# A graph kernel's edge sorter: ranks counted partition by partition, and one index copy for four scatters

## The chip, the cores and the metric

One core of a Trainium2 chip runs the kernel. The metric is the device time of one execution in microseconds (us). The engines named here are PE (matmuls; PEld is its weight loads), DVE (the vector engine), ACT (the scalar engine), POOL (here mostly the issuer of indirect scatters) and SP (the issuer of most transfers). Each engine takes its instructions in program order.

## What is computed

The graph has 12,500 nodes of 64 features and 200,000 edges, which come sorted by destination. Two graph layers follow one another, each with a residual:

```python
edge_index = jnp.stack([src, dst])
h = jnp.maximum(_layernorm(x, axis=-1), 0.0)
x = x + _L0_gnn_ref(h, edge_index, W1l, W1r, b1, W2l, W2r, b2)   # two SAGE convolutions
h = jnp.maximum(_layernorm(x, axis=-1), 0.0)
x = x + _L1_gnn_ref(h, edge_attr_64, src, dst, W1, b1, W2, b2)   # edge messages, mean by sender

def _sage_conv(x, src, dst, Wl, Wr, b):
    agg = jax.ops.segment_sum(x[src], dst, num_segments=N)
    cnt = jax.ops.segment_sum(jnp.ones((src.shape[0],), x.dtype), dst, num_segments=N)
    mean = agg / jnp.maximum(cnt, 1.0)[:, None]
    return mean @ Wl.T + b + x @ Wr.T
# messages: msg = relu([h[src], h[dst], edge] @ W1 + b1) @ W2 + b2, then the mean by src
```

## The kernel before

Nodes are cut into 49 blocks of 256. A *cell* is a pair of a destination block and a source block; there are 49 x 49 = 2401 of them, and each has 128 *slots* for its edges. Gathers and segment sums are matmuls with one-hot matrices, made from a slot's source number and destination number. So every edge first has to be given a slot: its rank among the edges of its cell.

**The stages.** From 0 to 92 us the node features are normalised and the first block is sorted. From 92 to about 1340 us runs the first convolution, with the sorter beside it; up to about 2305 us the second convolution; then two passes over the messages (`last` 0 and 1), with 40 early blocks and 9 late ones. In a convolution the cells go in groups of four (`some_cells`): eight matmuls gather into `got` (L896), ACT copies them to `rows` (L900), DVE makes the one-hot `hot` (L750) from `dcol`, and three groups later eight matmuls add into `acc` (L775). Every sixteen cells DVE makes two `turned` matrices (L741) from `srow`, a row of slot numbers that comes back from memory. When a destination block is complete, `conv` runs its chain over DVE, PE (L834, L839), ACT and DVE (L841).

**The sorter.** `sort(B)` is a generator of 14 steps (`STEPS`), and `sort_to` advances it between groups so that it stays about two blocks ahead; with 49 cells in a block, that is about one step per group. A block's edges lie in a window of 128 partitions x 34 (T = 34, pairs TG = 17). The steps:

- L594 compares the edges' source blocks with the 49 block numbers: a one-hot of 17 x 49 x 2 per partition (1666 elements).
- 17 matmuls (L598) count each column's edges of each cell; a scan and a multiply-add (L602, L603) make running counts, and L606 spreads them over a diagonal (`wide`).
- four pairs of matmuls (L616 with the triangle `lead`, L617 with `wide`) add what lies before an edge in its column and in earlier columns; ACT copies each result to `ranks` (L618), four copies.
- L620, twice, multiplies the one-hot by the source and the destination numbers.
- L625, twice, and L628 take the minimum over the 49 cells: the rank. L630 makes its bf16 copy.
- L635, twice, makes the one-hot of the ranks, `hot_r`. 34 matmuls (L645), with the cells' one-hot as weights (98 columns) and `hot_r` moving (128 columns), put each edge's numbers into its slot; in between L650 and L651 compute `pos`, the row that the edge's term takes in a table in memory.
- ACT copies the result to `rows_o` (L654), three transfers store it, PE transposes it (L663), and ACT writes `scol` and `dcol` (L664, L666).

All PSUM tiles of the sorter have the name `pX`, which has a single bank.

**The scatters.** `edge_terms` transforms edge features and scatters them to tables in memory (`terms`), in units of four tiles of early blocks (U = 4), or three of late ones. It runs as a generator that `Beside` advances at a fixed pace (4.45 per step, later 6.2). Each unit gives eight scatters (or six): for each, DVE copies one column of `pos` to `turn_i` (L381; 16 buffers of one column), and POOL issues an indirect transfer (L382). A unit's scatters go out during the steps of the next unit; those of the last unit of a phase are drained all at once:

```python
for _ in before:
    pass
```

In the message passes POOL also does the subtractions on `hidden` (L1089), which PE's sums (L775) need, and the `terms_in` loads read the tables back.

Of the kernel before, what the change touches and what calls it, by code (L numbers as in the profile page):

```python
# [9 lines left out]
FT = mybir.dt.float32  # L10
BF = mybir.dt.bfloat16
# [103 lines left out]
def fast_path(  # L115
# [239 lines left out]
    def edge_terms(work, psum, groups, ITEMS, U):  # L355
# [17 lines left out]
        def scatter(o, unit):  # L373
            for h in range(2):
                for c, (B, tg, _) in enumerate(unit):
                    assert sorted_blocks() > B
                    t = 2 * tg + h
                    j, n, _ = table_of(B)
                    assert j in cleared
                    at = work.tile([P, 1], I32, name="turn_i", bufs=16)  # L380
                    nc.vector.tensor_copy(at, pos_of(B)[:, t:t + 1])  # L381
                    nc.gpsimd.indirect_dma_start(  # L382
                        out=terms[j][:], out_offset=bass.IndirectOffsetOnAxis(ap=at, axis=0),
                        in_=o[:, c, h], in_offset=None,
                        bounds_check=S * NB * n - 1, oob_is_err=False)
                    yield
# [38 lines left out]
        for _ in before:  # L425
            pass
# [74 lines left out]
    def pos_of(B):  # L501
        return pos[:, B] if B < EARLY else pos_late[:, B - EARLY]
# [3 lines left out]
    def made_cells(work, psum):  # L506
# [8 lines left out]
        with tc.tile_pool(name="made", bufs=1, side="right") as made_in:  # L515
            kexp = made("kexp", [P, NB, 2], BF, [[1, NB], [0, 2]], -NB, 0)
            rexp = made("rexp", [P, S, 2], BF, [[1, S], [0, 2]], 0, 0)
            off = made("off", [P, NB, 1], FT, [[BLK, NB], [0, 1]], -1, 0)

            own = work.tile([P, NB, 2], BF, name="own", bufs=1)  # L520
            even_p = work.tile([P, 1], FT, name="even_p", bufs=1)
            diag_i = made_in.tile([P, NB, 2], I32, name="diag_i")
            nc.gpsimd.iota(diag_i, pattern=[[2, NB], [0, 2]], base=0, channel_multiplier=-1)
            here = made_in.tile([P, NB, 2], FT, name="here")
            nc.vector.tensor_scalar(here, diag_i, 0.0, None, op0=OP.is_equal)
            nc.vector.tensor_reduce(even_p, here.rearrange("p k c -> p (k c)"), AX.X, OP.max)
            nc.vector.tensor_scalar(own, diag_i, -1.0, None, op0=OP.is_equal)
            nc.vector.tensor_add(own, own, here)
            gap_i = made_in.tile([P, P], I32, name="gap_i")
            nc.gpsimd.iota(gap_i, pattern=[[1, P]], base=0, channel_multiplier=-1)  # L530
            lead = work.tile([P, P], BF, name="lead", bufs=1)
            nc.vector.tensor_scalar(lead, gap_i, 0.0, None, op0=OP.is_gt)
            gap = made_in.tile([P, P], BF, name="gap")
            nc.vector.tensor_scalar(gap, ident, -float(S), None, op0=OP.mult)
            nc.vector.tensor_add(lead, lead, gap)
        ones = work.tile([P, P], BF, name="ones", bufs=1)
        nc.vector.memset(ones, 1.0)
        before = [work.tile([2 * NB, TG + 1, 2], BF, name=f"before{n}", bufs=1) for n in range(2)]
        for b in before:
            nc.vector.memset(b, 0.0)  # L540
        flat_ones = work.tile([2 * NB, TG], FT, name="flat_ones", bufs=1)
        nc.vector.memset(flat_ones, 1.0)
        total = work.tile([2 * NB, NB], BF, name="total", bufs=1)
        batch = {}

        def edges_in(B0, B1, queue, i=None):
# [12 lines left out]
            kv, slo, dlo = (work.tile([P, CH, T], BF, name=k)[:, :n] for k in ("kv", "slo", "dlo"))  # L559
# [9 lines left out]
            nc.vector.scalar_tensor_tensor(kv, hi, -float(NB), f[:, 1], op0=OP.add, op1=OP.mult)  # L569
            nc.vector.tensor_scalar(hi, i[:, 0], BLK - 1, None, op0=OP.bitwise_and)  # L570
            nc.vector.tensor_scalar(slo, hi, 1.0, None, op0=OP.add)
            for B in range(B0, B1):
                batch[B] = tuple(t[:, B - B0] for t in (kv, slo, dlo))
# [12 lines left out]
        def flat(a):  # L586
            return a.rearrange("p g k c -> p g (k c)")

        def sort(B):

            kv, slo, dlo = batch[B]
# [4 lines left out]
            many = psum.tile([P, 512], FT, name="pX")  # L596
            for g in range(TG):
                nc.tensor.matmul(many[:2 * NB, g:g + 1], v[:, g, 0].rearrange("p k c -> p (k c)"), ones[:, 0:1],  # L598
                                 start=True, stop=True)
            yield  # L600
            b = before[B % 2]
            nc.vector.tensor_tensor_scan(b[:, 1:, 0], flat_ones, many[:2 * NB, :TG], 0.0, op0=OP.mult, op1=OP.add)  # L602
            nc.vector.scalar_tensor_tensor(b[:, 0:TG, 1], many[:2 * NB, :TG], even_p[:2 * NB], b[:, 0:TG, 0],  # L603
                                           op0=OP.mult, op1=OP.add)
            w = work.tile([2 * NB, TG, NB, 2], BF, name="wide", bufs=1)
            nc.vector.tensor_mul(w, mid(b[:, 0:TG], NB), lead_(own[:2 * NB], TG))  # L606
            nc.vector.tensor_copy(total[:, B:B + 1], b[:, TG, 0:1])


            r = work.tile([P, TG, NB, 2], BF, name="ranks", bufs=1)  # L610
            for n, g0 in enumerate(range(0, TG, 5)):
                yield
                g1 = min(g0 + 5, TG)
                p = psum.tile([P, 512], FT, name="pX")
                q = p[:, :(g1 - g0) * 2 * NB].rearrange("p (g k) -> p g k", k=2 * NB)
                nc.tensor.matmul(q, lead, flat(v[:, g0:g1, 0]), start=True, stop=False)  # L616
                nc.tensor.matmul(q, ones[:2 * NB], flat(w[:, g0:g1]), start=False, stop=True)  # L617
                nc.scalar.copy(flat(r[:, g0:g1]), q)  # L618
                if n % 2:
                    nc.vector.tensor_mul(v[:, :, 1 + n // 2], v[:, :, 0], mid(pairs((slo, dlo)[n // 2]), NB))  # L620
            yield
            k = NB
            for _ in range(2):
                h = k - k // 2
                nc.vector.tensor_tensor(r[:, :, 0:k - h], r[:, :, 0:k - h], r[:, :, h:k], op=OP.min)  # L625
                k = h
            rank = work.tile([P, T], FT, name="rank", bufs=1)
            nc.vector.tensor_reduce(pairs(rank), r[:, :, 0:k].rearrange("p g k c -> p g c k"), AX.X, OP.min)  # L628
            rb = work.tile([P, T], BF, name="rank_b", bufs=1)
            nc.vector.tensor_scalar(rb, rank, float(S), None, op0=OP.add)  # L630
# [9 lines left out]
            for g0, g1, hot in halves:  # L640
                yield

                for g in range(g0, g1):
                    for c in range(2):
                        nc.tensor.matmul(p[:2 * NB, :S], v[:, g, 1:3, :, c].rearrange("p v k -> p (v k)"),  # L645
                                         hot[:, g - g0, :, c], start=g + c == 0, stop=g + c == TG)
                if g0 == 0:
                    j, n, f = table_of(B)
                    q = work.tile([P, T], FT, name="pos_f", bufs=1)
                    nc.vector.scalar_tensor_tensor(q, rank, float(NB), kv, op0=OP.mult, op1=OP.add)  # L650
                    nc.vector.tensor_scalar(pos_of(B), q, float(n), float(n * (S * NB + NB) + f),  # L651
                                            op0=OP.mult, op1=OP.add)
            o = work.tile([2 * NB, S], BF, name="rows_o")
            nc.scalar.copy(o, p[:2 * NB, :S])  # L654
            yield
            n, f = place[B]
            F = len(order[n])
            nc.sync.dma_start(srow_b[B].rearrange("(k s) -> k s", s=S), o[0:NB])
            nc.sync.dma_start(srow_k[n][:, f * S:(f + 1) * S], o[0:NB])
            nc.sync.dma_start(drow_k[n][:, f * S:(f + 1) * S], o[NB:2 * NB])  # L660
            p = psum.tile([P, 512], FT, name="pX")
            pt = p.bitcast(BF)[:, 0:2 * NB]
            nc.tensor.transpose(pt, o, ident_b[:2 * NB, :2 * NB])  # L663
            nc.scalar.copy(scol[:, scol_at[n]:scol_at[n] + NB * F].rearrange("p (k f) -> p k f", f=F)[:, :, f],  # L664
                           pt[:, 0:NB])
            nc.scalar.copy(dcol[:, B * NB:(B + 1) * NB], pt[:, NB:])  # L666
# [17 lines left out]

        p = psum.tile([P, 512], FT, name="pX")
        nc.tensor.matmul(p[:NB, :NB], own[:2 * NB, :, 0], total, start=True, stop=True)
        most = work.tile([NB, 1], FT, name="most", bufs=1)
        nc.vector.tensor_reduce(most, p[:NB, :NB], AX.X, OP.max)
        p = psum.tile([P, 512], FT, name="pX")
        nc.tensor.transpose(p[0:1, :NB], most, ident[:NB, :NB])  # L690
        flag = work.tile([1, 1], FT, name="flag", bufs=1)
        nc.vector.tensor_reduce(flag, p[0:1, :NB], AX.X, OP.max)
        nc.vector.tensor_scalar(flag, flag, S + 0.5, None, op0=OP.is_gt)
        nc.vector.tensor_max(bad, bad, flag)

    STEPS = 14
# [731 lines left out]
```

## Time and profile before

| | |
|---|---|
| median of 3 runs | 3727.71 us (3725.05 to 3731.02) |
| the profiled execution | 3723.96 us, span 3722.1 us, mean granted PE clock 0.991 |
| busy share of the span | PE 94%, PEld 92%, DVE 89%, ACT 69%, POOL 73% |
| L381, index copies | 1360 of early blocks (169.1 us listed), 306 of late ones |
| L382, scatters | 1666, 1937.7 us listed on POOL |
| L618, rank evictions on ACT | 147 of 490 columns (568 ns), 49 of 196 (333 ns) |
| L645, slot matmuls | 1666, 224 ns listed each |

A listed duration of PE or DVE runs from the start of an instruction to its end, and instructions of one engine overlap a little; the distance from one start to the next says how long the engine is held. The profile names, for each wait, the engine and line whose end released it.

### The profile page before, as it was taken

The numbers are of one execution on the slowest core, as the hardware profiler recorded it, in microseconds if no ns is written. First come the engines' busy times: TensorE is split into PE (matmuls) and PEld (weight loads), VectorE is DVE, ScalarE is ACT, GpSimd is POOL, SyncE is SP. The second block draws the span as 40 slices with busy tenths as digits, with TensorE's granted clock in tenths as the row PEclk, the third lists the DMA queues.
The fourth block names the chain that finished last, engine by engine and source line by source line (L and its number), as shares of the span: only waits on it lengthen the run. The fifth ranks groups of instructions, "written<-read, shape, count | busy, mean of one in ns | idle before, by whom it ended". The sixth has DMA issues, their size and how long they took to land.

```text
span 3722.1 us, 130679 instructions
## 1 busy us (share of the span) xinstructions
PE 3505.5 (94%) x51318; PEld 3423.2 (92%) x51318; DVE 3322.8 (89%) x7346; ACT 2568.7 (69%) x5875; POOL 2732.6 (73%) x2306
## 2 busy tenths in 40 slices
PE   1799999999999999999999998999999999998987
PEld 0799999999999999999999998899999999998887
DVE  7899999999999978888888887899999999998998
ACT  3466666666666667777777776688888888876665
POOL 4057787777778777777777774688888888996454
PEclk9999999999999999999999999999999999999999
DMA  6654555555454344444444444666666666666664
GB/s 209 247 169 148 159 153 157 156 157 156 137 166 151 116 129 141 136 136 144 136 131 140 139 132 131 227 215 203 217 214 212 203 216 210 208 196 193 196 213 138
DMA packets 413697, 635.90 MB, mean 171 GB/s; under 512 B 94131, under 2 KB 296247, under 8 KB 413070
## 3 DMA queue, kind: packets, MB, share of 16 engines
q1 hardware_dynamic: 353106, 572.87, 48.7%
q0 software_dynamic: 53312, 51.36, 4.6%
q8 instruction: 402, 6.59, 0.7%
q10 hardware_dynamic: 6652, 3.24, 0.4%
q14 instruction: 225, 1.84, 0.2%
HBM read 474.72 MB, written 155.83 MB: 169 GB/s over the span
## 4 chain that ended last, share of the span: by engine, by line
PE 75%; DVE 15%; DMA 4%; issue 3%; ACT 2%; POOL 1%; SPq 1%; DVEq 0%; POOLq 0%; ACTq 0%
PE acc L775 26%; PE got L896 17%; PE got L1077 11%; PE got L1078 6%; PE pE L414 4%; DVE hot L750 3%; DVE turned L741 2%; PE pE L399 2%; DVE hot_r L635 2%; PE pX L645 2%; DVE turned_d L741 1%; DMA terms_in<-terms 1%; PE acc L839 1%; PE got L1074 1%; PE pX L617 1%
## 5 line engine op out<-in xcount | busy, mean ns | idle before, releaser
L382 POOL DMA_INDIRECT terms<-terms_o,turn_i x1666 | 1937.7, 1163 | 663.3 <-issue 220.5
L900 ACT CAST rows<-got 128x384 bf16<-128x384 f32 x2402 | 1038.5, 487 | 592.3 <-PE got L896 577.7
L775 PEld LDWEIGHTS <-hot 128*128 128x128 bf16 x12006 | 1029.5, 98 | 19.0 <-issue 7.9
L775 PE MATMUL acc<-rows,hot 128*128 128x193 bf16 x9604 | 1006.0, 247 | 0.7 <-DVE hot L750 0.7
L1089 POOL TENSOR_TENSOR hidden<-hidden 128x512 f32<-128x512 f32 (+1 forms) x602 | 756.3, 1257 | 259.6 <-ACT hidden L1086 179.3
L896 PEld LDWEIGHTS <-turned 128*128 128x128 bf16 x9604 | 814.7, 98 | 67.4 <-issue 27.5
L750 DVE TENSOR_TENSOR hot<-dcol,local 128x1024 bf16<-128x1024 bf16 x1202 | 814.3, 682 | 4.1 <-PE acc L775 3.7
L741 DVE TENSOR_SCALAR turned<-srow,nid 128x2048 bf16<-128x2048 bf16 (+1 forms) x906 | 780.4, 875 | 21.1 <-issue 10.7
L1077 PE MATMUL got<-ta,turned 128*128 128x128 bf16 x3920 | 599.8, 220 | 7.3 <-DVE turned L741 7.3
L1077 PE MATMUL got<-tb,turned_d 128*128 128x128 bf16 x3920 | 600.7, 221 | 1.7 <-DVE turned_d L741 1.1
L1078 PE MATMUL got<-tb,turned_d 128*128 128x64 bf16 x3920 | 546.9, 193 | 0.0
L1078 PE MATMUL got<-ta,turned 128*128 128x64 bf16 x3920 | 546.5, 193 | 0.0
L896 PE MATMUL got<-ta,turned 128*128 128x192 bf16 x4802 | 499.7, 247 | 37.4 <-issue 24.8
L1097 ACT ACTIVATE hot_a<-every,scol 128x256 bf16<-128x256 bf16 x1200 | 507.0, 493 | 0.0
L896 PE MATMUL got<-tb,turned 128*128 128x192 bf16 x4802 | 494.1, 246 | 0.8 <-DVE turned L741 0.5
L1086 ACT ACTIVATE hidden<-y 128x512 f32<-128x512 f32 (+1 forms) x301 | 190.4, 632 | 293.5 <-DVE y L1083 169.5
L1077 PEld LDWEIGHTS <-turned 128*128 128x128 bf16 x3920 | 362.8, 98 | 8.2 <-issue 7.8
L1077 PEld LDWEIGHTS <-turned_d 128*128 128x128 bf16 x3920 | 360.2, 98 | 2.9 <-DVE turned_d L741 2.4
L1078 PEld LDWEIGHTS <-turned 128*128 128x128 bf16 x3920 | 359.5, 98 | 1.2
L1078 PEld LDWEIGHTS <-turned_d 128*128 128x128 bf16 x3920 | 359.9, 98 | 0.0
L741 DVE TENSOR_SCALAR turned_d<-drow,nid 128x2048 bf16<-128x2048 bf16 (+2 forms) x302 | 324.9, 1117 | 0.0
L1099 ACT ACTIVATE hot_a<-hot_a 128x1024 bf16<-128x1024 bf16 x300 | 317.2, 1057 | 9.5
(227 smaller groups left out, 5302.4 us busy)
## 6 DMA issues: line engine op xcount, KB each, us to landing
srow<-srow_b SPq DMA_DIRECT2D x300, 512.0 KB
srow<-srow_k SPq DMA_DIRECT2D x149, 512.0 KB
drow<-drow_k SPq DMA_DIRECT2D x149, 512.0 KB
terms_in<-terms SPq DMA_DIRECT2D x294, 160.0 KB
edges<-in_edge_attr_dram SPq DMA_DIRECT2D x200, 192.0 KB
terms<-tb SPq DMA_DIRECT2D x200, 160.0 KB
terms<-tb SPq DMA_DIRECT2D x48, 640.0 KB
terms<-terms_o,turn_i POOLq DMA_INDIRECT x1666
```

What stands on the lines that cost most here:

```text
L382: nc.gpsimd.indirect_dma_start(out=terms[j][:], out_offset=bass.IndirectOffsetOnAxis(ap=at, axis=0), in_=o[:, c, h], in_offset=None, bound ...
L741: nc.vector.tensor_scalar(o[:, h, :n * S], r[:, :n * S], nid[:, h:h + 1], None, op0=OP.is_equal)
L750: nc.vector.tensor_tensor(o[:, :n], cols.rearrange("p (g c) -> p g c", c=2).unsqueeze(2).to_broadcast([P, n, 2 * P, 2]), local.rearrange(" ...
L775: nc.tensor.matmul(self.acc[B][:, h, :W3], lt, r[:, c, 0:W3], start=k + h == 0, stop=k == row - 1 and h == 1, skip_group_check=True)
L896: nc.tensor.matmul(p[:, (i - c) * D3:(i - c + 1) * D3], t[:, h, (a - c0 + i) * S:(a - c0 + i + 1) * S], table[:, (a + i) % NB, h], start=h ...
L900: nc.scalar.copy(g[:, c:c + m, :D3], p[:, :m * D3].rearrange("p (c d) -> p c d", c=m))
L1077: nc.tensor.matmul(p[:, c], lt, rt[:, 0:2 * D], start=i == 0, stop=False, skip_group_check=True)
L1078: nc.tensor.matmul(p[:, c, 0:D], lt, rt[:, 2 * D:], start=False, stop=i == 3, skip_group_check=True)
L1086: nc.scalar.activation(w[:, :n, 0:D], y[:, :n], AF.Relu)
L1089: nc.gpsimd.tensor_sub(w[:, :n, (i + 1) * D:(i + 2) * D], w[:, :n, j], upper(w)[:, :n, j])
L1097: nc.scalar.activation(q[:, c - k], every, AF.Abs, scale=-1.0, bias=scol[:, scol_at[last] + a + c:scol_at[last] + a + c + 1])
L1099: nc.scalar.activation(q[:, :n - k], q[:, :n - k], AF.Relu, bias=1.0, scale=-2.0)
```

## The change

The sorter now ranks an edge in another order: first all edges of its cell in earlier partitions, then those before it in its own partition.

- The 17 counting matmuls and the four pairs become 17 matmuls with the triangle `lead` as weights and the cells' one-hot moving (98 columns), all summed into one PSUM tile: how many edges of each cell lie in earlier partitions. `ahead_p` is that sum over the two columns of a pair, read from PSUM by DVE.
- Within a partition, DVE compares each edge's key with the 33 keys before it. The keys lie in a buffer of 67 columns, 33 of padding and 34 of keys, and `earlier` is an overlapping view of it. Edges outside the block get the key 8192, which takes one more instruction per seven blocks.
- The product of one-hot and `ahead_p` and the comparisons lie side by side in `ranks` (49 + 33 pairs); three halving adds and a reduce sum them. A running maximum (`most`) replaces the counts for the overflow test.
- In the slot matmuls the weights are now `hot_r` (128 columns), and the cells' one-hot moves (98 columns). The result comes out transposed, so `scol` and `dcol` are written at once and the transpose makes `rows_o`. The three transfers are issued in the same step as that transpose.
- A block takes 13 steps instead of 14.
- For early blocks, one DVE copy takes the four columns of a half unit, and four scatters read it; late blocks keep a copy for each scatter. The last unit's scatters are yielded one by one.

```diff
         def scatter(o, unit):
             for h in range(2):
-                for c, (B, tg, _) in enumerate(unit):
+                B0, t = unit[0][0], 2 * unit[0][1] + h
+                if B0 < EARLY:
+                    four = work.tile([P, len(unit)], I32, name="turn_i", bufs=4)
+                    nc.vector.tensor_copy(four, pos[:, B0:B0 + len(unit), t])
+                for c, (B, _, _) in enumerate(unit):
...
-                    at = work.tile([P, 1], I32, name="turn_i", bufs=16)
-                    nc.vector.tensor_copy(at, pos_of(B)[:, t:t + 1])
+                    if B0 < EARLY:
+                        at = four[:, c:c + 1]
+                    else:
+                        at = work.tile([P, 1], I32, name="turn_i", bufs=16)
+                        nc.vector.tensor_copy(at, pos_of(B)[:, t:t + 1])
...
         for _ in before:
-            pass
+            yield
...
+        def earlier(a):
+            (row, _), (step, _) = a.ap
+            return bass.AP(a.tensor, a.offset, [[row, P], [2 * step, TG], [step, T - 1], [step, 2]])
...
-            many = psum.tile([P, 512], FT, name="pX")
+            p = psum.tile([P, 512], FT, name="pX")
+            q = p[:, :2 * NB].rearrange("p (k c) -> p k c", c=2)
             for g in range(TG):
-                nc.tensor.matmul(many[:2 * NB, g:g + 1], v[:, g, 0].rearrange("p k c -> p (k c)"), ones[:, 0:1],
-                                 start=True, stop=True)
+                nc.tensor.matmul(q, lead, v[:, g, 0], start=g == 0, stop=g == TG - 1)
+            r = work.tile([P, TG, KE, 2], BF, name="ranks", bufs=1)
+            nc.vector.tensor_tensor(r[:, :, NB:], mid(pairs(kv), T - 1), earlier(keyed), op=OP.is_equal)
             yield
-            b = before[B % 2]
-            nc.vector.tensor_tensor_scan(b[:, 1:, 0], flat_ones, many[:2 * NB, :TG], 0.0, op0=OP.mult, op1=OP.add)
-            nc.vector.scalar_tensor_tensor(b[:, 0:TG, 1], many[:2 * NB, :TG], even_p[:2 * NB], b[:, 0:TG, 0],
-                                           op0=OP.mult, op1=OP.add)
-            w = work.tile([2 * NB, TG, NB, 2], BF, name="wide", bufs=1)
-            nc.vector.tensor_mul(w, mid(b[:, 0:TG], NB), lead_(own[:2 * NB], TG))
-            nc.vector.tensor_copy(total[:, B:B + 1], b[:, TG, 0:1])
-            r = work.tile([P, TG, NB, 2], BF, name="ranks", bufs=1)
-            for n, g0 in enumerate(range(0, TG, 5)):
-                yield
...
-                nc.tensor.matmul(q, lead, flat(v[:, g0:g1, 0]), start=True, stop=False)
-                nc.tensor.matmul(q, ones[:2 * NB], flat(w[:, g0:g1]), start=False, stop=True)
-                nc.scalar.copy(flat(r[:, g0:g1]), q)
-                if n % 2:
-                    nc.vector.tensor_mul(v[:, :, 1 + n // 2], v[:, :, 0], mid(pairs((slo, dlo)[n // 2]), NB))
+            nc.vector.tensor_mul(v[:, :, 1], v[:, :, 0], mid(pairs(slo), NB))
             yield
-            k = NB
-            for _ in range(2):
+            ahead_p = work.tile([P, NB, 2], BF, name="ahead_p", bufs=1)
+                nc.vector.tensor_reduce(ahead_p, q.unsqueeze(2).to_broadcast([P, NB, 2, 2]), AX.X, OP.add)
+            nc.vector.tensor_mul(r[:, :, 0:NB], v[:, :, 0], lead_(ahead_p, TG))
+            yield
+            nc.vector.tensor_mul(v[:, :, 2], v[:, :, 0], mid(pairs(dlo), NB))
+            yield
+            k = KE
+            for n in range(3):
                 h = k - k // 2
-                nc.vector.tensor_tensor(r[:, :, 0:k - h], r[:, :, 0:k - h], r[:, :, h:k], op=OP.min)
+                nc.vector.tensor_tensor(r[:, :, 0:k - h], r[:, :, 0:k - h], r[:, :, h:k], op=OP.add)
                 k = h
-            rank = work.tile([P, T], FT, name="rank", bufs=1)
-            nc.vector.tensor_reduce(pairs(rank), r[:, :, 0:k].rearrange("p g k c -> p g c k"), AX.X, OP.min)
+                if n == 1:
+                    yield
             rb = work.tile([P, T], BF, name="rank_b", bufs=1)
-            nc.vector.tensor_scalar(rb, rank, float(S), None, op0=OP.add)
+                nc.vector.tensor_reduce(pairs(rb), r[:, :, 0:k].rearrange("p g k c -> p g c k"), AX.X, OP.add)
+            nc.vector.tensor_max(most, most, rb)
...
                     for c in range(2):
-                        nc.tensor.matmul(p[:2 * NB, :S], v[:, g, 1:3, :, c].rearrange("p v k -> p (v k)"),
-                                         hot[:, g - g0, :, c], start=g + c == 0, stop=g + c == TG)
+                        nc.tensor.matmul(p[:, :2 * NB].rearrange("p (v k) -> p v k", v=2), hot[:, g - g0, :, c],
+                                         v[:, g, 1:3, :, c], start=g + c == 0, stop=g + c == TG)
...
-            o = work.tile([2 * NB, S], BF, name="rows_o")
-            nc.scalar.copy(o, p[:2 * NB, :S])
-            yield
+            cols = work.tile([P, 2 * NB], BF, name="cols_o")
+            nc.scalar.copy(cols, p[:, :2 * NB])
+            nc.scalar.copy(scol[:, ...], p[:, 0:NB])
+            nc.scalar.copy(dcol[:, B * NB:(B + 1) * NB], p[:, NB:2 * NB])
+            yield
+            nc.tensor.transpose(pt, cols, ident_b)
+            o = work.tile([2 * NB, S], BF, name="rows_o", bufs=1)
+            nc.scalar.copy(o, pt)
             nc.sync.dma_start(srow_b[B].rearrange("(k s) -> k s", s=S), o[0:NB])
...
-    STEPS = 14
+    STEPS = 13
```

In the prediction, L596, L605, L609 and similar numbers that do not occur above are lines of the changed kernel: L596 the one-hot of the cells, L601 the 17 matmuls, L603 the comparison, L605 and L612 the two products with the numbers, L609 `ahead_p`, L610 its product, L617 the adds, L623 the reduce.

## The prediction

> **What bounds the kernel now.** I read the busy table by stages first, because the sorter runs only inside the first convolution. Columns: stretch and its length, then busy us (instructions) of PE, PEld, DVE, ACT and POOL, the granted clock, the DMA share, GB/s.
>
> ```profile
> 92.00:210.00 118.00, 96.82 (x1068) 87.11 (x1068) 100.83 (x194) 58.09 (x146) 0.99 (x1) 0.99 0.68 238
> 210.00:1190.00 980.00, 941.60 (x11090) 904.31 (x11089) 916.67 (x2345) 626.59 (x1570) 765.69 (x622) 1.00 0.51 155
> 1190.00:1300.00 110.00, 106.63 (x1265) 102.73 (x1264) 102.44 (x267) 71.59 (x181) 87.31 (x71) 1.00 0.37 115
> 1345.00:2290.00 945.00, 945.00 (x10736) 934.00 (x10734) 792.26 (x2305) 683.39 (x1843) 709.31 (x637) 1.00 0.43 136
> ```
>
> The second convolution (1345 to 2290) is PE alone: 945 of 945 us, so DVE work saved there buys nothing. In the sorting stretch (210 to 1190, 39 blocks) PE and DVE are both nearly full, and each waits for the other. The waits of DVE in that stretch (us in total, times, longest) come next:
>
> ```profile
> DVE ranks L625 <- ACT ranks L618: 26.7, 28, 2.1
> DVE conv L841 <- PE acc L839: 13.3, 16, 2.7
> DVE before L602 <- PE pX L598: 2.1, 6, 0.8
> ```
>
> With 5.6 us of smaller ones that is 48 us. DVE is therefore held for 980 - 48 = 932 us (917 busy, the rest gaps between dependent instructions). PE waits 38 us and is held for 942.
>
> Prices must be start to start, since a short instruction overlaps its neighbour. The timeline of DVE inside one block (start, us):
>
> ```profile
> 506.18 0.21 DVE L381 COPY turn_i<-pos 128x1 int32<-128x1 int32 x2
> 506.30 0.68 DVE L750 TENSOR_TENSOR hot<-dcol,local 128x1024 bf16<-128x1024 bf16 x1
> ...
> 523.65 1.02 DVE L625 TENSOR_TENSOR ranks<-ranks 128x816 bf16<-128x816 bf16 x2
> 524.71 0.61 DVE L628 TENSOR_REDUCE rank<-ranks 128x34 f32<-128x442 bf16 x1
> 525.35 0.18 DVE L630 TENSOR_SCALAR rank_b<-rank 128x34 bf16<-128x34 f32 x1
> ```
>
> Two index copies hold DVE for 0.12 us, 0.06 each, though one is listed at 0.15. The two dependent minima hold it for 1.06 and the reduce for 0.64; a 1666-element tensor_tensor (L594, listed at 1.02) starts at 510.90 with its successor at 511.84, so 0.94. For PE, the same stage and one later stretch:
>
> ```profile
> 504.01 1.21 PE L645 MATMUL pX<-hot_r,hot 128*98 128x128 bf16 x18
> 505.05 0.60 PE L399 MATMUL pE<-ident,edges 128*128 128x128 f32 x4
> ...
> 516.42 0.37 PE L616 MATMUL pX<-hot,lead 128*128 128x490 bf16 x1
> 516.63 0.37 PE L617 MATMUL pX<-wide,ones 98*128 98x490 bf16 x1
> 516.84 0.82 PE L896 MATMUL got<-ta,turned 128*128 128x192 bf16 x8
> ...
> 2699.99 0.22 PE L1077 MATMUL got<-ta,turned 128*128 128x128 bf16 x1
> 2700.05 0.19 PE L1078 MATMUL got<-ta,turned 128*128 128x64 bf16 x1
> 2700.08 0.22 PE L1077 MATMUL got<-ta,turned 128*128 128x128 bf16 x1
> ```
>
> Eighteen slot matmuls take 1.04 us, 58 ns each, with 98-column weights; a 490-column one takes 210 ns; with 128-column weights a 128-column matmul starts its successor after 57 ns and a 64-column one after 29.
>
> **PE and ACT, per block.** Removed: 17 counts (L598) at 46 ns, 0.78; three pairs at 0.42 and one 196-column pair at 0.17 (L616, L617), 1.43; 34 slot matmuls at 58 ns, 1.96; together 4.17. Added: 17 + 34 matmuls with 128-column weights and 98 moving columns. Between the 29 and 57 ns rows that is 44 ns each, 2.25. The transpose stays at 0.05. PE saves 1.9 us a block, 75 us in the stretch: 942 becomes 867. ACT loses the four rank evictions (3 x 0.57 + 0.33) and gains one more 98-column copy of about 0.3, so 1.7 us less, off the path.
>
> **DVE, per block.** Unchanged: L594, both L620, both L635, L650, L651. Removed: L602 0.22, L603 0.28, L606 0.94, L607 0.06, L625 1.03 (mean of its pairs), L628 0.64, L630 0.10; 3.27. Added, at 0.51 ns per element (816 elements are listed at 585 ns, 1666 at 1021), with 0.09 for an instruction that nothing waits for (L594: 0.94 less 0.85) and 0.2 for one whose result the next needs (L625: 1.03 less 0.63 for 1224 elements, halved): the comparison over 17 x 66 = 1122 elements, 0.66; the sum over PSUM, 196 elements at 1.02 ns (L628 442 at 614, L325 896 at 1077) plus 0.2, 0.41; the product into the ranks, 0.94; adds of 1394, 680 and 340 elements, 0.91, 0.55 and 0.37; the reduce of 374, 0.57; the running maximum, 0.10; the second key instruction, 0.3 per seven blocks, 0.04. Together 4.55, so DVE gains 1.28 us a block, 50 us in the stretch.
>
> **Index copies.** The trace has 624 in the stretch; three in four go, 468 x 0.063 = 29 us. DVE becomes 932 + 50 - 29 = 953 us. Of the other 736 copies of early blocks some 75 lie between 1190 and 1300; the rest lie in the PE-only convolution and count as nothing. If DVE bound there, three quarters of them would be worth 31 us, but DVE waits 141 us of it. The merged copy waits for a buffer of four scatters instead of one, which queues the hot and sort work behind it. POOL, 766 of 980 busy, itself waits for the copies, so I add nothing, at worst 3 us.
>
> **Where the stall goes.** The 26.7 us behind the evictions and the 2.1 behind L598 lose their producers. In their place L609 waits for the 17 matmuls, two DVE instructions after PE could start them: covered by the comparison and L605, 1.6 us against 0.75. What is late next is conv behind PE; with PE 75 us lighter I keep half of the 13.3 and all 5.6 of the small ones: 12 us. The stretch becomes 953 + 12 = 965, a gain of 15. The single pX bank is now held until three ACT copies are done (about 1 us), a wait for PE, which has 98 us to spare.
>
> **Start and end of the sort.** From 92 to 210 there are five blocks: DVE +6.4, waits -8.6, so -2. From 1190 to 1300 PE is the fuller, four blocks: PE -7.6, DVE +5.2 less 3.5 of copies; I take -2. Three setup instructions and the shorter overflow test are below 1 us each.
>
> **The late scatters.** The last yields change the other end. Today six scatters go out in one burst, and the hidden work queues behind them on POOL:
>
> ```profile
> PE acc L775 <- POOL hidden L1089: 6.8, 1, 6.8
> ```
>
> Spread at the pace before the burst (1.3 a group of 4.1 us, where PE waited for nothing), they end some 19 us later, near 3397, just before the next table loads (3407, or 3400 without the stall). I take -7, between -9 (the matmuls after the stall run at half speed for 3 us) and 0 (the loads then wait for the last scatter).
>
> **The sum.** -15 - 2 - 2 - 7 = -26 us. The profiled execution took 3723.96 us (span 3722.1), 3.7 below the median of the runs; applied to the median, 3727.71 - 26 = 3702.
>
> [...] No row of before starts a 16-bit operand of DVE on an odd element. The keys are 67 wide with the live part at 33, so the comparison and L596 in four blocks of seven would. [...]
>
> **Rivals.** *Odd operands at one element per step* (0.17, and the one that ends slower). At 1.02 ns per element the comparison costs 0.58 more, and L596 0.84 more in four of seven blocks, 0.48. That is 1.06 a block: 41 us in the stretch, 994 + 12 = 1006, a loss of 26 there; start and end turn to +3 and +2, late -7: about 3752. It decides from 0.55 us a block beyond my sum. Against it: every tensor_tensor of bf16 here, stride-zero pairs included, lies near 0.5 ns, and L594 is the nearest shape, so I take its rate. *The waits stay* (0.15): the sum in PSUM or the conv chain takes the place of the evictions, 33 us instead of 12. The stretch is 986, start and end give nothing, and with -7 late the whole is 3727. For it: conv waited 16 times with PE only half the cause. *PE alone was the bound* (0.08): all DVE waits close, so 953 flat (-27), -7 at start and end, -9 late: 3685. For it: PE's lines hold most of the chain in this stretch; against it: DVE cannot go below 953.
>
> **How the numbers follow.** The forecast has 0.60; its own range, with 0.25 us a block either way for the short adds and 0 to 9 late, is 3684 to 3719. The odd case reaches past 3742, the last rival to 3684; 3684 to 3742 leaves out about 0.2. About 0.2% (7 us) is what a measurement of this kernel can tell from no change. Faster by more: 0.55 of the forecast and the 0.08, 0.63. Same: 0.11 of the second rival and 0.04 of the forecast, 0.15. Slower: 0.17, 0.04 and 0.01, 0.22.
>
> **What would show it.** Right: the comparison near 0.74 us listed, slot matmuls near 44 ns apart, DVE above 96% of the sorting stretch with no wait above 15 us in total, PE near 90%, no POOL burst near 3380. Wrong: a comparison near 1.3 us, hot of L596 in two lengths, or a new DVE wait on pX or acc of 25 us.

## The result, and the profile after

The changed kernel takes 3739.44 us (median of 17 runs, 3732.00 to 3747.93) against 3727.79 us for the kernel before beside it (17 runs, 3725.05 to 3734.19): a ratio of 1.003, 95% interval 1.0023 to 1.0037. The forecast was 3702, so the change is slower where it was to be faster. The profiled execution took 3739.99 us (span 3738.1), 16 us more than the one before. In the runs of experiments 9 to 12, of their repeats and of a first try of 13 the kernel before itself took 4194 to 4197 us, so their times compare with no others; beside all other runs it took 3726 to 3729.

Where the 16 us lie is read from three landmarks: the last reciprocal of the first convolution (`rcnt`, L821), the last gather sum of the second (L769) and the message passes. The first convolution ends at 1370 us instead of 1348, 22.5 later. The second takes as long as before. The first message pass, from its first to its last gather (L1077 before, L1071 after), is 6.4 us shorter (1075.3 against 1081.7), the second about as long as before.

Busy time by stages of the changed kernel (stretch and length; busy us and instructions of PE, PEld, DVE, ACT, POOL; clock; DMA share; GB/s):

```profile
92.00:210.00 118.00, 91.65 (x1052) 86.10 (x1053) 113.07 (x200) 50.92 (x133) 2.22 (x2) 0.91 0.69 237
210.00:1190.00 980.00, 876.95 (x10538) 851.18 (x10536) 950.19 (x1842) 550.80 (x1422) 767.17 (x609) 0.98 0.50 151
1190.00:1300.00 110.00, 101.10 (x1233) 98.78 (x1232) 108.11 (x205) 64.77 (x167) 88.44 (x70) 0.98 0.41 124
1345.00:2290.00 945.00, 944.17 (x10718) 932.94 (x10716) 763.45 (x1828) 681.28 (x1835) 708.17 (x643) 1.00 0.43 135
```

In the sorting stretch PE fell from 942 to 877 us and DVE rose to 950, 97% of it, although it issues 500 instructions fewer. Its waits in that stretch (us in total, times, longest):

```profile
DVE conv L835 <- PE acc L833: 12.9, 11, 2.6
DVE turned L735 <- DMA srow<-srow_b: 3.6, 2, 2.5
```

The 27 us behind the rank evictions are gone and nothing took their place. DVE bounds the stretch, as the forecast said; it has more to do than the forecast said. The one-hot and the comparison, over the whole run (lowest, median and highest duration in ns):

```profile
L596 DVE TENSOR_TENSOR hot<-keys,kexp x49: 1010/1879/1886, 19.2 to 1290.2; 128x1666 bf16<-128x1666 bf16 x49
L603 DVE TENSOR_TENSOR ranks<-keys x49: 1028/1309/1319, 22.9 to 1293.3; 128x1122 bf16<-128x1122 bf16 x49
```

The median of L596 is far above its lowest value. The timeline shows why: two lengths, by the block. First a block whose live keys start on an odd element, then the next one, where they start on an even one (start, us):

```profile
510.58 1.89 DVE L596 TENSOR_TENSOR hot<-keys,kexp 128x1666 bf16<-128x1666 bf16 x1
512.38 1.31 DVE L603 TENSOR_TENSOR ranks<-keys 128x1122 bf16<-128x1122 bf16 x1
```

```profile
538.84 1.02 DVE L596 TENSOR_TENSOR hot<-keys,kexp 128x1666 bf16<-128x1666 bf16 x1
...
541.31 1.04 DVE L603 TENSOR_TENSOR ranks<-keys 128x1122 bf16<-128x1122 bf16 x1
```

The same instruction of the same size takes 1.89 or 1.02 us. A row of keys is 67 elements and the live part begins at 33, so four rows of seven put it on an odd element: 28 blocks of 49. The comparison has two lengths too, and neither is the 0.74 that the prediction named.

### The profile page after: what moved, and what is told of

It is laid out like the page before. It is cut to its first block, busy times and chain, and to the rows that moved or that the text cites. A ratio compares the mean times of both kernels' runs of the same rounds, so it can differ in the third digit from the quotient of the medians.

```text
span 3738.1 us, 128406 instructions
## 1 busy us (share of the span) xinstructions
PE 3443.0 (92%) x50925; PEld 3379.6 (90%) x50925; DVE 3368.5 (90%) x6327; ACT 2488.7 (67%) x5728; POOL 2748.1 (74%) x2305
## 4 chain that ended last, share of the span: by engine, by line
PE 63%; DVE 21%; DMA 6%; issue 5%; POOL 2%; SPq 2%; ACT 1%; DVEq 0%; POOLq 0%; ACTq 0%
PE acc L769 22%; PE got L890 13%; PE got L1071 12%; PE got L1072 6%; DVE hot L744 4%; PE pE L421 3%; DVE turned L735 3%; DMA terms<-terms_o,turn_i 3%; DVE hot_r L629 2%; POOL terms L389 2%; DVE turned_d L735 2%; PE pE L406 2%; DVE ranks L617 1%; DVE hot L596 1%; PE got L1068 1%
## 5 line engine op out<-in xcount | busy, mean ns | idle before, releaser
L769 PEld LDWEIGHTS <-hot 128*128 128x128 bf16 x12006 | 1036.1, 99 | 15.9 <-issue 5.3
L769 PE MATMUL acc<-rows,hot 128*128 128x193 bf16 x9604 | 1014.6, 248 | 0.3 <-DVE hot L744 0.3
L890 PE MATMUL got<-ta,turned 128*128 128x192 bf16 x4802 | 515.5, 250 | 99.4 <-DVE turned L735 98.0
L1071 PE MATMUL got<-ta,turned 128*128 128x128 bf16 x3920 | 599.4, 220 | 7.2 <-DVE turned L735 7.2
L1071 PE MATMUL got<-tb,turned_d 128*128 128x128 bf16 x3920 | 600.7, 220 | 3.2 <-DVE turned_d L735 2.1
L1071 PEld LDWEIGHTS <-turned 128*128 128x128 bf16 x3920 | 362.6, 98 | 8.1 <-issue 7.7
L1071 PEld LDWEIGHTS <-turned_d 128*128 128x128 bf16 x3920 | 359.8, 98 | 4.7 <-DVE turned_d L735 3.2
```

The source lines that it names most:

```text
L769: nc.tensor.matmul(self.acc[B][:, h, :W3], lt, r[:, c, 0:W3], start=k + h == 0, stop=k == row - 1 and h == 1, skip_group_check=True)
L890: nc.tensor.matmul(p[:, (i - c) * D3:(i - c + 1) * D3], t[:, h, (a - c0 + i) * S:(a - c0 + i + 1) * S], table[:, (a + i) % NB, h], start=h ...
L1071: nc.tensor.matmul(p[:, c], lt, rt[:, 0:2 * D], start=i == 0, stop=False, skip_group_check=True)
```

## The experiments

**1. Even key rows.** The changed kernel with rows of 68 and the live part at column 34:

```diff
-        keys = [work.tile([P, CH, 2 * T - 1], BF, ...)]
+        keys = [work.tile([P, CH, 2 * T], BF, ...)]
-            kv = keyed[:, T - 1:]
+            kv = keyed[:, T:]
-            return bass.AP(a.tensor, a.offset, [[row, P], ...])
+            return bass.AP(a.tensor, a.offset + step, [[row, P], ...])
```

> The key rows get 68 columns instead of 67 and the live part begins at column 34, so every pair of keys that L596 reads starts on an even element; in the comparison of L603 the live part is even too, but half of its 33 windows still start odd. Theory (each bf16 pair that starts on an odd element costs DVE more, and DVE is the bound of the sorting stretch): L596 takes 1.02 us in all blocks instead of 1.88 in 28 of 49, L603 1.04 us in all instead of 1.31 in those 28; 28 x 0.87 + 28 x 0.27 = 32 us less for DVE, and the time falls from 3739 to about 3708, 3720 if half of it turns into waits for PE. Rival (the two lengths come from something else that alternates with the blocks, such as the copies or transfers beside them): both lengths stay and the time is 3739 within 4. Second rival (the lengths go but PE's chain through hot and hot_r is the bound): L596 at 1.02 and the time still within 6 us of 3739.

Measured: 3723.14 us (3720.22 to 3727.66; ratio to before 0.9987, 0.9978 to 0.9996), 16 below the changed kernel. The lengths are as the theory has them in all 49 blocks:

```profile
L596 DVE TENSOR_TENSOR hot<-keys,kexp x49: 1011/1018/1029, 18.9 to 1269.9; 128x1666 bf16<-128x1666 bf16 x49
L603 DVE TENSOR_TENSOR ranks<-keys x49: 1028/1036/1043, 21.8 to 1272.2; 128x1122 bf16<-128x1122 bf16 x49
```

So the odd start makes both long lengths. But 32 us of DVE's time went and only 16 us of the run's. Waits of DVE in the first convolution (90 to 1375 us) of this kernel:

```profile
DVE turn_i L379 <- DMA terms<-terms_o,turn_i: 29.2, 15, 4.1
DVE conv L835 <- PE acc L833: 16.0, 11, 3.2
```

The merged index copy waits 29 us for a buffer whose four scatters have not all landed. In the changed kernel the same wait was 7.5 us.

**2. The odd start alone, in the kernel before.** Its keys `kv` at column 1 of rows of 36, nothing else:

```diff
+            kv = work.tile([P, CH, T + 2], BF, name="kv")[:, :n, 1:T + 1]
-            kv, slo, dlo = (work.tile([P, CH, T], BF, name=k)[:, :n] for k in ("kv", "slo", "dlo"))
+            slo, dlo = (work.tile([P, CH, T], BF, name=k)[:, :n] for k in ("slo", "dlo"))
```

> The kernel before with its keys kv kept at column 1 of rows of 36, so that every pair that L594 reads starts on an odd element; no other part of the change, no overlapping view. Theory (an odd start is the cause by itself): L594 goes from 1.02 to about 1.88 us in all 49 blocks, 0.87 x 39 = 34 us more for DVE between 210 and 1190, where it waits 48 us and keeps about 17 of waits when it is the bound: 3 to 34 us longer, 3731 to 3765, likeliest 3740. Rival (the odd start matters only together with the rows of 67 or the overlapping view): L594 stays at 1.02 and the time at 3728 within 4.

Measured: 3769.64 us (ratio 1.0114, 1.0097 to 1.0131), 40.5 above the kernel before, more than the range. The one-hot line, L595 here:

```profile
L595 DVE TENSOR_TENSOR hot<-kv,kexp x49: 1876/1882/1891, 19.2 to 1310.0; 128x1666 bf16<-128x1666 bf16 x49
```

It was 1014 to 1028 ns before. So neither the overlapping view nor the rows of 67 are needed; the odd start does it. 49 x 0.86 = 42 us of DVE work became 40.5 us of time: DVE's waits absorbed next to nothing; between 210 and 1190 us they are still 45 us, against 48. The scatters grew as well, from 1.23 to 1.30 us in the mean of that stretch; how much of the 40.5 us is theirs was not separated.

**3. Index copies back to one for each scatter**, the rest as changed:

```diff
-                    four = work.tile([P, len(unit)], I32, name="turn_i", bufs=4)
-                    nc.vector.tensor_copy(four, pos[:, B0:B0 + len(unit), t])
...
+                    at = work.tile([P, 1], I32, name="turn_i", bufs=16)
+                    nc.vector.tensor_copy(at, pos_of(B)[:, t:t + 1])
```

> The change with one index copy for each scatter again (16 buffers of one column) instead of one for four; all else as changed. Theory (DVE bounds the sorting stretch, a copy holds it for 0.063 us): 468 copies more between 210 and 1190 us, and some 100 beside it, 29 to 35 us longer in the first convolution, nothing in the second: 3768 to 3774. Rival (the copies fell in gaps of DVE, so that taking them away was worth nothing): 3739 within 5. Third (the merged copy's wait for a buffer of four scatters costs something itself): below 3739.

Measured: 3766.86 us (ratio 1.0102, 1.0087 to 1.0118), 27 above the changed kernel, and the first convolution ends 25.5 later. In a kernel that DVE bounds, the copies are worth about what the forecast took.

**4. The last scatters in one burst again** (`pass` for `yield` in the last drain), the rest as changed:

> The change without the yields behind the last blocks: the last scatters go out in one burst as before; all else as changed. Theory (the burst delays the hidden work on POOL near the end of the first message pass): a wait of PE for POOL's hidden of about 6.8 us returns and the first message pass is 6 to 7 us longer, 3746. Rival (the shorter message pass of the change came from other data in the tables' queues): 3739 within 2.

Measured: 3747.76 us (ratio 1.0053, 1.0039 to 1.0067), 8 above the changed kernel. In the first message pass PE's wait is back:

```profile
PE acc L769 <- POOL hidden L1083: 8.1, 1, 8.1
```

**5. Even rows and eight buffers** for the merged copies (`bufs=8` for `bufs=4`):

> Even key rows as in the first experiment, and eight buffers instead of four for the merged index copies. With even key rows alone DVE waited 29 us in the first convolution for a merged copy's buffer (7.5 in the change, 2.1 with single copies), and only 15 us of the 32 taken off DVE were seen. Theory (a buffer of four is free only when all four of its scatters have landed, so 12 instead of 15 scatters can be under way; twice the buffers close that wait): the wait falls below 5 us, and the time to 3698 to 3705. Rival (the scatters' own pace on POOL is the limit, 1.09 us each and 0.3 between two): the wait goes elsewhere in DVE's or ACT's order and the time stays at 3720 to 3726.

Measured: 3717.08 us (ratio 0.9971, 0.9959 to 0.9983), between the theory and its rival. DVE no longer waits for those buffers. But now ACT does for the data of the scatters, of which it has three buffers; its wait between 210 and 1190 us:

```profile
ACT terms_o L429 <- DMA terms<-terms_o,turn_i: 42.1, 20, 4.9
```

In the kernel before and in the changed kernel this line does not occur. The wait moved more than it closed: the scatters themselves come no faster, 617 in the stretch, against 619 in experiment 1.

**6. Every start even.** As 5, with a second copy of the keys, moved by one column, so that the 17 windows that started odd are read from it:

```diff
-            nc.vector.tensor_tensor(r[:, :, NB:], mid(pairs(kv), T - 1), earlier(keyed), op=OP.is_equal)
+            nc.vector.tensor_tensor(r[:, :, NB:NB + TG], mid(pairs(kv), TG), earlier(shifted, TG), op=OP.is_equal)
+            nc.vector.tensor_tensor(r[:, :, NB + TG:], mid(pairs(kv), TG - 1), earlier(keyed, TG - 1), op=OP.is_equal)
```

> As the fifth experiment, and the keys are kept a second time, moved by one column, so that the comparison goes in two instructions, 17 windows from the moved copy and 16 from the first, and every pair starts on an even element. The shifted source ids take the place of the destination ids in their tile to make room. Theory (the comparison's 1.04 us with even rows is the price of the half of its windows that start odd): the two take about 0.38 and 0.36 us listed, 0.74 in sum as forecast for the single one, some 0.2 to 0.3 less per block start to start, 10 to 14 us over 49 blocks, less 1 to 2 for the extra copies: 8 to 12 us below the fifth. Rival (the overlapping view itself is slow, whatever the start): 1.04 or more in sum, and the time 2 to 8 us above the fifth.

Measured: 3707.39 us (3706.12 to 3717.08; ratio 0.9949, 0.9936 to 0.9961), 10 below the fifth and the fastest kernel of this study, ahead of both. The two comparisons:

```profile
L608 DVE TENSOR_TENSOR ranks<-keys,moved x49: 445/455/466, 22.0 to 1256.5; 128x578 bf16<-128x578 bf16 x49
L609 DVE TENSOR_TENSOR ranks<-keys x49: 428/436/468, 22.3 to 1256.9; 128x544 bf16<-128x544 bf16 x49
```

Listed they sum to 0.89, not the 0.74 expected, because each has its own end; the next instruction follows 0.09 us before an end, so together they hold DVE for about 0.7 us, against 0.96 for the one with odd windows (541.31 to 542.27 in the changed kernel).

**7. The sum over PSUM off DVE.** As 6, but PE adds both slots of a pair (34 matmuls of 49 columns), ACT copies `ahead_p`, and the product with the destination goes ahead of the product into the ranks:

```diff
+                for c in range(2):
+                    nc.tensor.matmul(q, lead, v[:, g, 0, :, c], start=g + c == 0, stop=g + c == TG)
-                nc.vector.tensor_reduce(ahead_p, q.unsqueeze(2).to_broadcast([P, NB, 2, 2]), AX.X, OP.add)
+            nc.scalar.copy(ahead_p, q.unsqueeze(2).to_broadcast([P, NB, 2]))
```

> As the sixth, and the sum over PSUM of L609 leaves DVE: PE adds both slots of a pair itself (34 matmuls of 49 columns instead of 17 of 98), ACT copies the sum out, and the product with the destination stands ahead of the product that needs it. Theory (DVE is the bound of the sorting stretch and PE has slack): DVE is 0.39 us per block lighter, 19 us over 49 blocks, PE up to 0.6 us heavier inside its 100 us of idle time: 12 to 19 us below the sixth. Rival (PE's chain or the wait for PE and ACT ahead of the product eats it): within 6 us of the sixth, with a new wait of DVE on ahead_p of 10 us or more.

Measured: 3756.67 us (3742.88 to 3775.51; ratio 1.0078, 1.0054 to 1.0101), 49 above the sixth. Neither the theory nor its rival holds: DVE is lighter (897 us busy in the stretch instead of 944, with 3% less done in it), and neither PE nor ACT is late with `ahead_p`. The scatters are late. ACT's wait for their data between 210 and 1190 us is now

```profile
ACT terms_o L429 <- DMA terms<-terms_o,turn_i: 89.4, 28, 7.2
```

and in that stretch POOL makes 594 scatters at a mean of 1.32 us, against 623 at 1.25 in the sixth. What stands behind `terms_o` on ACT is then late as well: between 90 and 1375 us DVE waits 59 us at `conv` for PE's sums, against 23 in the sixth. One of the long scatters, with the longer of DVE's instructions beside it:

```profile
455.36 5.45 POOL L389 DMA_INDIRECT terms<-terms_o,turn_i  x1 [0.30 <-issue]
...
455.66 1.02 DVE L612 TENSOR_TENSOR hot<-hot,slo 128x1666 bf16<-128x1666 bf16 x1
...
456.60 0.69 DVE L750 TENSOR_TENSOR hot<-dcol,local 128x1024 bf16<-128x1024 bf16 x1
...
457.20 1.02 DVE L616 TENSOR_TENSOR hot<-hot,dlo 128x1666 bf16<-128x1666 bf16 x1
...
458.13 0.69 DVE L750 TENSOR_TENSOR hot<-dcol,local 128x1024 bf16<-128x1024 bf16 x1
...
458.94 1.03 DVE L618 TENSOR_TENSOR ranks<-hot,ahead_p 128x1666 bf16<-128x1666 bf16 x1
...
459.87 0.75 DVE L741 TENSOR_SCALAR turned<-srow,nid 128x2048 bf16<-128x2048 bf16 x1
```

The scatter begins beside the products and is over at 460.81, 0.84 us after the last of these `tensor_tensor` instructions ended (458.94 + 1.03 = 459.97). That is no accident: all 88 scatters of this stretch that last 1.6 us or more end 0.77 to 0.87 us after the end of some `tensor_tensor` of DVE, as do all 70 in the sixth, while only one instant in eight lies so. In the sixth the sum over PSUM, a `tensor_reduce`, stands ahead of the product into the ranks; here one `tensor_tensor` follows another at once.

**8. PE's relief taken back.** As 5, with the 17 count matmuls issued twice (`for again in range(2)` around them):

> As the fifth experiment, but the 17 matmuls of the count ahead are issued twice in a row, the second set starting the sum anew, so that PE gets back 17 x 44 ns = 0.75 us per block, 37 us over 49 blocks. Theory (DVE alone bounds the sorting stretch; PE's relief bought nothing by itself): 0 to 8 us above the fifth. Rival (PE still sets part of the pace, so that its relief was worth its half): 15 us or more above the fifth.

Measured: 3722.29 us (ratio 0.9984, 0.9974 to 0.9994). 37 us of PE work cost 5 us. PE does not set the pace of this kernel.

**9 to 12, without a verdict.** Four kernels were meant to separate the scatters from DVE: the sixth and the seventh with the scatters' pace changed as below (9 and 10), the seventh with a pause on DVE (11), and the kernel before at the new pace (12).

```diff
-                beside.passed((z - a) * (1.1, 0.9)[layer])
+                beside.passed((z - a) * (1.0, 1.0)[layer])
...
+            nc.vector.tensor_copy(pause[:, 4:8], pause[:, 0:4])
+            nc.vector.tensor_copy(pause[:, 8:12], pause[:, 4:8])
```

> As the sixth experiment (3707), and the planner that issues the scatters beside the two convolutions goes at (1.0, 1.0) of its pace instead of (1.1, 0.9): 9% fewer scatters in the first convolution, 11% more in the second, the same number in sum. Theory (with DVE relieved, the scatter stream on POOL is nearly full in the first convolution, 775 us of 980 and 0.24 us between any two, and costs it some of the gain): 10 to 20 us off the first convolution, where the index copies also go down by 9%, 0 to 5 us on the second: 3690 to 3702. Rival (POOL had room; only the index copies count): 4 us or less below the sixth.

> As the seventh experiment (3757, with the sum over PSUM off DVE), at the pace (1.0, 1.0). There ACT waited 89 us for the data of earlier scatters between 210 and 1190 us and POOL made only 594 scatters in that stretch at 1.32 us each, against 623 at 1.25 in the sixth. Theory (the scatter stream became the bound of the seventh): 9% fewer scatters in the first convolution are worth up to 9% of its 980 us there, until DVE is the bound again: 3700 to 3720, 35 us or more below the seventh. Rival (the new wait for PE and ACT ahead of the product is what costs the 49 us): within 12 us of the seventh.

> As the seventh experiment (3757), and two tiny copies of 4 columns on DVE, the second of which needs the first, between the product with the destination and the product into the ranks: some 0.3 us more of DVE's time per block, 15 us over 49. Theory (DVE's products back to back keep POOL from ending a scatter, and the removed sum over PSUM was such a pause): the mean scatter between 210 and 1190 us falls from 1.32 us towards 1.25, and the time to 3715 to 3740 in spite of the added work. Rival (no such pause counts): the mean stays at 1.32 within 0.02 and the time at 3757 or up to 15 us above.

> The kernel before at the pace (1.0, 1.0), a control for the ninth. Theory (before is held by DVE and PE together, and 9% fewer scatters take 56 index copies of 0.063 us off DVE): 3 to 8 us below the kernel before, so that a gain of the ninth over the sixth beyond that belongs to POOL. Rival (before was held by the scatter stream too): 15 us or more below.

Measured beside a kernel before of 4194.06 us: 4258.73, 4314.76, 4291.95 and 4211.90 us, ratios of 1.0152, 1.0294, 1.0229 and 1.0040. The tenth and the eleventh were run twice more, at 4316 and 4321, and at 4298 and 4291, beside 4197. The sixth and the seventh were not run there, so nothing follows from these times: what the scatters cost the seventh rests on its profile. The traces give a hint on the pause. Between 210 and 1190 us the mean scatter is 1.25 to 1.26 us in the tenth and its two repeats and 1.19 to 1.22 in the eleventh and its two. But the two kernels also differ in pace, and POOL is idle for over 200 us of that stretch there beyond its usual gaps, so this is no test.

**13. The small parts alone, in the kernel before**: merged copies with four buffers and the last yields, with the old ranking. (A first try beside 4197 took 4341.)

> The kernel before with the two small parts of the change alone (one index copy for four scatters, the yields behind the last blocks), once more, since the kernel before itself took 4197 us beside the first try. Theory (before passes DVE's work on to the time one to one): the copies are worth 27 to 30 us there too, the yields 8, less up to 20 us of waits for a merged copy's buffer: 3692 to 3705, below the sixth experiment's 3707, so that the new ranking costs more than the old even with every start even. Rival (the copies are worth something only where the new ranking has made DVE the bound): 3715 to 3722, the yields and little else.

Measured: 3723.71 us (3717.42 to 3731.68; ratio 0.9994, 0.9985 to 1.0003), 3 below the kernel before, so the rival is nearer. The yields were worth some 8 in experiment 4; if they are here too, the copies were worth less than nothing, and the first convolution does end at 1359 instead of 1348. DVE is 28 us less busy in the stretch, and waits in the first convolution (90 to 1345 us):

```profile
DVE ranks L631 <- ACT ranks L624: 37.7, 33, 3.5
DVE conv L847 <- PE acc L845: 29.8, 31, 3.5
DVE turn_i L378 <- DMA terms<-terms_o,turn_i: 29.2, 20, 4.0
```

The third line is new against the kernel before and is as long as what was saved. The wait for `conv` grew too, from 23 us.

## Why the prediction was wrong, point by point

**The step that failed: the price of the one-hot and the comparison.** The forecast took 0.94 and 0.66 us a block, at the rate of the nearest rows. From start to start they held DVE for 1.43 and 1.11, 0.95 more in sum, 47 us over 49 blocks. The first rival said 1.06 more, and named the two lengths of L596 and a comparison near 1.3 us as what would show it; they are there. The cause it named was right and its price nearly so: what is paid is 1.04 ns for each pair that starts odd. L596 has 833 pairs and pays 0.87. The comparison has 561, and 0.74 us is its estimate at the rate of the even rows; with odd keys all pay (0.74 + 0.58 = 1.32, measured 1.31), with even keys the 289 of the odd windows do (0.74 + 0.30 = 1.04, measured 1.04). The rival had missed this last part. It gave 0.17 to the case on the ground that every product of bf16 lay near 0.5 ns; but no row of before reads a pair from an odd element, so those rows could not speak on it. (The prediction says that no 16-bit operand starts odd there; L603 of before does write one from an odd element on, but every second element, with no pair in it.) The case deserved the larger share.

**What the experiments settle.** Nothing in the profile of before could say whether the start counts; experiments 1, 2 and 6 do. A one-hot of 1666 elements takes 1.02 us from even starts in all 49 blocks (experiment 1) and 1.88 from odd ones, also in the kernel before (experiment 2), and the comparison holds DVE for about 0.7 us instead of 0.96 once every start is even (experiment 6). That holds for operands whose inner run is two elements. Longer runs were not tried.

**The second failing step: "POOL, 766 of 980 busy, itself waits for the copies, so I add nothing, at worst 3 us".** Busy time left out some 0.3 us between any two scatters. In the sixth experiment, with 1.25 us each, 623 of them fill 966 us of 980. Before, 622 at 1.23 already filled some 955, and POOL seldom waited for a copy: a scatter there starts 7 us (median) after its own copy has ended. No kernel here made more than 623 in the stretch, whatever was taken off DVE. In the changed kernel DVE was slower still, and POOL kept up with it: of four scatters that share a copy, the first starts 3.0 us (median) after the copy, and the merged copy's wait was 7.5 us. As soon as DVE is relieved, POOL falls behind: 12.0 us after the copy in experiment 1, 14.6 in experiment 5, 18.3 in experiment 7, 14.3 in experiment 13. The wait is then 29 us at the copy (experiments 1 and 13), or 42 at ACT (experiment 5). So the forecast's 965 us for the stretch would probably not have come about by its own means either: of the 32 us of odd starts that experiment 1 removed, half returned.

**The other terms.** PE got lighter, though by less than taken. The 877 us measured in the stretch look like the forecast's 867, but the slower kernel does some 2% less in it; over the whole first convolution PE's busy time fell by 56 us (1192 to 1136), where the forecast's 1.92 us a block make 94. The slot matmuls follow one another after 51 ns in the mean, not 44, the 17 count matmuls after 46, and the granted clock was 0.97 there instead of 1.00; how much each took was not separated, and with DVE as the bound it cost no time. The remaining DVE terms were within 0.12 us (forecast in brackets): `ahead_p` 0.39 (0.41), its product 0.95 (0.94), adds 1.71 (1.83), reduce 0.58 (0.57), maximum 0.10 (0.10). DVE's waits: 17 us against 12. PE alone as the bound: refuted, since PE got lighter and the kernel slower, and by experiment 8. The copies: 27 us (experiment 3) against 29, where DVE is the bound. The late scatters: 6.4 us by the profile, 8 by experiment 4, against 7.

**The sum again.** The changed kernel is 37 us above the forecast. Even rows take 16 off, more buffers 6, even windows 10: 3707, 5 above the forecast, with the scatters as what is late next.

## What to carry to other kernels

Before a DVE operand gets a new layout, work out on which element each of its inner runs starts, in every row: an odd row length changes that from row to row (here one instruction took 1.02 or 1.88 us by the block), and rows of the old profile that all start even say nothing of it. An engine that issues indirect scatters can be full at a busy share of 78%, as POOL was here before the change (766 of 980 us); count its instructions, add the gap between two of them (some 0.3 us here), and give it a price of its own. When one buffer serves four transfers it comes free with the last of them, so the number of buffers has to grow when the copies are merged: DVE waited 29 us for four such buffers in experiment 1 and not at all for eight in experiment 5.

## What was not expected of the hardware

A pair of bf16 elements that starts on an odd element costs DVE 1.04 ns more than one that starts even, in a `tensor_tensor` with inner runs of two (1.88 against 1.02 us for 1666 elements), and by the two lengths of the comparison (1.31 and 1.04 us) it is paid once even where both inputs start odd.

Scatters that POOL issues get longer beside DVE's products: 1.25 us in the mean in the first convolution of the sixth experiment, 1.32 in the seventh and 1.11 in the second convolution of either, up to 5.45 us where products follow one another. In the traces of the sixth and the seventh the long ones, of 1.6 us or more, lie beside `tensor_tensor` and end 0.77 to 0.87 us after one has ended, whatever follows it: a `tensor_scalar`, an index copy or a `tensor_tensor` that needs its result. What holds a scatter until then was not shown. The odd one-hot lasts 0.87 us longer, which may be why the scatters grew in experiment 2; that was not tested.
